# Loads of a pair at the first step in every batch, sums inverted a step later, and a longer run of unread products before the first expert

## The chip, the cores and the metric

One core of one Trainium2 chip runs the whole program; the other cores are idle. The metric is the device time of one execution in microseconds (us). TensorE (PE, with its weight loads PEld), VectorE (DVE), ScalarE (ACT), GpSimd (POOL) and SyncE (SP) each run their own instructions in order. Most transfers are issued by SP, some by ACT, the indirect ones by POOL.

## The reference

The input `x` has four batches of 1024 positions and 256 columns. A layer of attention with a normalization is followed by a layer of experts with a second normalization:

```
q, k, v = x wq^T, x wk^T, x wv^T             # 16 heads of 16 columns
q_embed = softplus(q) * (cos, sin of the position angles)
k_embed = softplus(k) * (cos, sin of the angles plus a bias)
x = layernorm(x + softmax(q_embed k_embed^T / 4) v wo^T)
gates = softmax(x router_w + router_b); the two best of 8 experts for each token
slots: each expert takes its first 640 tokens in order of position
y = sum over a token's experts of gate * (gelu(x w1 + b1) w2 + b2)
x = layernorm(x + y)
```

All is in float32.

## The kernel before

**Attention.** Work goes by units. A pair of heads of one batch is a unit of 8 steps; there are 8 pairs in a batch (the first four belong to the first half of the heads, the other four to the second) and 4 batches, so 256 steps in all. Pair p and step t of batch b are written (p, t) here. (The first and the last pair are cut into two units of 4 steps, which doesn't matter below.) In each step TensorE multiplies keys by queries (`key_scores`, L797), subtracts row maxima by a small product (L811), ScalarE takes exponentials (L818, two in each step, so that the start of the first of them marks the step), and TensorE multiplies the exponentials of the step before by the values (`weighted_values`, L838). The maxima are needed beforehand: `score_half` (L757) makes scores of a coming unit and VectorE reduces them to maxima (L761), four or so in every step. These score products of a unit may start at the last step of the pair two ahead of it; so they read the unit's `qk` tile from about (0, 6) or (0, 7) on if the unit is pair 2.

**The tiles of a pair.** `load_qk` (L471) brings a pair's embedded queries and keys from DRAM to a `qk` tile: 12 transfers on SP, 8 of 128 KB and 4 of 256 KB, 2 MB in all. There are three such buffers, so the tile of pair i takes the buffer of pair i - 3, and SP waits until that pair's last key scores are made. L1094 says at which step this is issued: at the first step of the pair two before it; but in the first pair of batches 1 to 3 at its fourth step (t = 3).

**Sums.** At the end of a unit `collect` (L856) sends six transfers on SP: numerators to `num` and sums to DRAM. When half of a batch's heads is done, `over_sums` (L879) runs in four pieces: it loads the sums as `den`; VectorE inverts them (L886), the result goes to DRAM (L888) and eight transfers spread it to `r` (L891); then two multiplications of `num` by `r` (L897). For the second half of the heads these pieces are placed at steps 1, 2, 5 and 6 of the first pair of the next batch (L947). `project` (L500) then multiplies by the output weights, from (0, 7) on, and VectorE adds the result (L514). For the first half of the heads the pieces stand at (4, 1), (4, 3) and two later steps; in the last batch at (4, 1), (4, 3), (4, 6) and (4, 7), where pair 6's tile is loaded at (4, 0).

**Order.** Within `tc.manual_schedule()` instructions go to the engines in the order of the program, and the table `todo` says what is added at which step.

**Experts.** After the last batch is routed, POOL scatters its rows to slots of the experts in DRAM by 16 indirect transfers (L692). `second_factors` (L703) computes `again`, the factors of the second normalization of the tokens that go to no expert. Then `slots_of(0, n=1)` (L1193) loads the 640 slots of the first expert as five tiles by five transfers on SP (L1198), which wait for all scatters; 34 products of `again` with the identity matrix go to an unread bank of PSUM (L1332, L1333; each is two records in the profile); `transposed` (L1201) turns each tile on TensorE (L1207) and ScalarE copies it (L1208); then TensorE multiplies by the first expert's weights (L1363, L1384), and so on through the eight experts.

Of the kernel before, what the change touches and what calls it, by code (L numbers as in the profile page):

```python
# [20 lines left out]
P = 128  # L21
# [7 lines left out]
def kernel(  # L29
# [18 lines left out]
    nc = tc.nc  # L48
    B, S, DIM = x.shape
    E, _, HID = w1.shape  # L50
    HD = 16
    NT = S // P
# [8 lines left out]
    ST = CAP // P  # L61
# [23 lines left out]
    again = keep.tile([P, B * NT], F32, name="again")  # L85

    ident = const.tile([P, P], F32, name="ident")
# [14 lines left out]
    with ExitStack() as actx:  # L102
# [750 lines left out]
        def by_rows(w):  # L853
            return units[w][1] < B - 1 or units[w][2] == 0
# [24 lines left out]
        def over_sums(b, f):  # L879

            num = nums.pop((b, f))
            width = 2 * FH * HS // P
            den = small.tile([P, width], F32, tag="den", name=f"den_{b}_{f}", bufs=1)
            nc.sync.dma_start(den, sums[b, f].rearrange("n m (c s) -> (n m c) s", s=width))
            yield
            nc.vector.reciprocal(den, den)  # L886
            over = dram.tile([2, FH, HS], F32, name=f"over_{b}_{f}")
            nc.sync.dma_start(over.rearrange("n m (c s) -> (n m c) s", s=width), den)  # L888
            r = p1.tile([P, 2, HS], F32, tag="os", name=f"r_{b}_{f}")
            for m in range(FH):  # L890
                nc.sync.dma_start(  # L891
                    r[HD * m : HD * (m + 1), :, :],
                    over[:, m, :].unsqueeze(0).to_broadcast([HD, 2, HS]),
                )
            yield
            for n in range(2):
                nc.vector.tensor_tensor(num[:, n, :], num[:, n, :], r[:, n, :], ALU.mult)  # L897
                ots[b, f, n] = num[:, n, :].rearrange("p (i t) -> p i t", t=P)
                yield
# [30 lines left out]
        def at(b, p, c, f, *args):  # L930
            todo.setdefault((b * NU + p) * NT + c, []).append((f, args))

        def run(pieces):
            next(pieces, None)
# [9 lines left out]

        for b in range(1, B):
            pieces = over_sums(b - 1, 1)
            for c in (1, 2, 5, 6):  # L947
                at(b, 0, c, run, pieces)
            for j, (p, c) in enumerate(((0, 7), (1, 0), (1, 1), (1, 2))):
                at(b, p, c, project, b - 1, 1, j)  # L950
            for j, (p, c) in enumerate(((1, 2), (1, 3), (1, 4), (1, 5))):
                at(b, p, c, statistics, b - 1, j)
# [39 lines left out]
        for w in range(1, len(units)):  # L992
            rows = range(16 if units[w][4] is None else 8)
# [3 lines left out]
            before = [starts[v] for v in range(w) if units[v][0] == units[w][0] - 1]  # L997
# [91 lines left out]
        with tc.manual_schedule():  # L1089
            for n in range(NS):  # L1090
                w, c = step_of[n]
                b, p, t = n // (NU * NT), n // NT % NU, n % NT

                if t == 0 and p > 0 or t == 3 and p == 0 and b > 0 or n == NT // 2:  # L1094
                    i = n // NT + 2
                    if i < B * NU:
                        load_qk(i)
                    elif i - B * NU < 2:
                        experts[i - B * NU] = expert_weights(i - B * NU)
                if n == NS - 2:  # L1100
                    turn_back(B - 1, 1, 0)


                third_last, others[0] = others[0], False
                items = [(score_half, *x) for x in ahead[n]]
                first, third, fourth, rest = items[:2], items[2:3], items[3:4], items[4:]
                if third_last:
                    third, fourth = [], third + fourth
                for f, *args in first:
                    f(*args)  # L1110
                if parts:
                    run(parts)
                    parts = None
                tiles = [key_scores(w, c, 0)]
                for f, *args in third:
                    f(*args)
                tiles.append(key_scores(w, c, 1))
                for f, *args in fourth:
                    f(*args)
                exponentials(w, c, tiles)  # L1120
                if n > 0:
                    weighted_values(*step_of[n - 1])
                for f, *args in rest:
                    f(*args)
                if n + 2 in starts:
                    parts = max_parts(starts.index(n + 2))
                    run(parts)
                if n + 1 in starts:
                    max_rows(starts.index(n + 1))
                if c == 1 and w > 0 and not by_rows(w - 1):  # L1130
                    normalize(w - 1)
                for f, args in todo.get(n, ()):
                    f(*args)
                if b > 0 and (p, t) in FINISH:
                    if b not in finishing:
                        finishing[b] = finish_batch(b - 1)
                    next(finishing[b], None)
                if n == NS - 2:
                    for j in range(2):
                        project(b, 1, j)  # L1140
                        statistics(b, j)
                    one, two = (
                        finish_batch(b, rotate=True, lo=lo, n=NT // 2) for lo in (0, NT // 2)
                    )
                elif n == NS - 1:
                    run(one)
            weighted_values(*step_of[NS - 1])


        with tc.manual_schedule():  # L1150
            b, n = B - 1, NT // 2
# [28 lines left out]
    with ExitStack() as mctx:  # L1180
# [9 lines left out]
        b2_sb = mconst.tile([P, E, DIM], F32, name="b2_sb")  # L1190
        nc.scalar.dma_start(b2_sb.rearrange("p e d -> p (e d)"), b2.partition_broadcast(P))

        def slots_of(e, by=nc.sync, n=ST):  # L1193

            s_sb = m2.tile([P, ST, ROW], F32, tag="slots", name=f"slots_{e}")
            rows = slots_in[e * CAP : (e + 1) * CAP, :].rearrange("(t p) d -> p t d", p=P)
            for t in range(0, ST, n):
                by.dma_start(s_sb[:, t : t + n, :], rows[:, t : t + n, :])  # L1198
            return s_sb

        def transposed(e, s_sb, t):  # L1201

            if t == 0:
                s_ts[e] = m2.tile([P, KC, CAP], F32, tag="slots_t", name=f"slots_t_{e}")
            ps = ps_t.tile([P, KC, P], F32, tag="t", name=f"st_{e}_{t}")
            for k in range(KC):
                nc.tensor.transpose(ps[:, k, :], s_sb[:, t, k * P : (k + 1) * P], ident)  # L1207
            nc.scalar.copy(s_ts[e][:, :, t * P : (t + 1) * P], ps)  # L1208
# [115 lines left out]

        y_views = dram_disjoint_views(y_rank, (E - 1) * ST)
        half = CAP // 2
        s_ts, tiles, before = {}, {0: slots_of(0, n=1)}, None
        with tc.manual_schedule():


            idle = ps_h.tile([P, 2, 512], F32, tag="h", name="idle")
            for _ in range(34):  # L1332
                nc.tensor.matmul(idle[0 : B * NT, 0, 0:P], again, ident, start=True, stop=True)  # L1333
            for t in range(ST):
                transposed(0, tiles[0], t)
            for e in range(E):
                w1_sb, w2_sb = experts.pop(e)
                s_sb, s_t = tiles.pop(e), s_ts.pop(e)
                if 0 < e < E - 1:
                    tiles[e + 1] = slots_of(e + 1)  # L1340
# [18 lines left out]
                for c in range(HC):  # L1359
                    ps = ps_h.tile([P, 2, 512], F32, tag="h", name=f"hp_{e}_{c}")  # L1360
                    for k in range(KC):
                        for i in range(2):
                            nc.tensor.matmul(  # L1363
                                ps[:, i, 0:half],
                                w1_sb[:, k, c * P : (c + 1) * P],
                                s_t[:, k, i * half : (i + 1) * half],
                                start=(k == 0),
                                stop=(k == KC - 1),
                            )
                    nc.scalar.activation(  # L1370
                        h_t[:, c, :].rearrange("p (i n) -> p i n", i=2),
                        ps[:, :, 0:half],
                        AF.Gelu,
                        bias=b1_sb[:, e, c : c + 1],
                    )
                    if e == 0 and c == 1:
                        tiles[1] = slots_of(1, nc.scalar)
                for t in range(ST):
                    if e + 1 < E and t > 0:
                        for i in (t - 1,) if t < ST - 1 else (t - 1, t):  # L1380
# [2 lines left out]
                    for c in range(HC):  # L1383
# [4 lines left out]
                            start=(c == 0),  # L1388
                            stop=(c == HC - 1),
# [22 lines left out]
                before = row, to  # L1412
# [70 lines left out]
```

## Time and profile before

| | |
|---|---|
| time, median of 5 runs | 1425.52 us (1420.96, 1420.99, 1425.52, 1426.52, 1428.54) |
| the profiled execution's own time | 1421.81 us |
| its span, first to last instruction | 1420.0 us |
| attention in it: first exponential to last | 43.7 to 1083.2 us |
| first product with an expert's weights | 1129.3 us |
| TensorE busy | 1370.6 us, 97% of the span |
| VectorE, ScalarE, GpSimd busy | 885.7, 738.8, 407.0 us |
| mean granted clock of TensorE | 0.987 |

Times in the views are in us from the first instruction. A row of a timeline gives start, length, engine, line, operation, names of what is written and read, count, and in brackets how long the engine had been idle before it and what ended this. PEclk is the granted share of TensorE's full clock.

### The profile page before, as it was taken

The page shows a single profiled execution, that of the slowest core. Times are in us where ns is not written, and L with a number is a line of the kernel's source. Part 1 is how long each engine was busy: PE and PEld are TensorE (multiplying, and loading weights), DVE is VectorE, ACT ScalarE, POOL GpSimd, SP SyncE. Part 2 cuts the span into 40 slices and gives each one's busy share as a digit, 9 for nine tenths or more (in the row PEclk, how much of TensorE's full clock was granted, in tenths as well). Part 3 has the DMA queues.
Part 4 walks back from the last instruction along what each step waited for, and adds up shares of the span by engine and source line. Part 5 has one row for each costly group of instructions (what it writes and reads, how often), then busy time and mean ns, then how long its engine had stood idle before and what let it go on. Part 6 is the DMA issues. An engine that isn't in the chain of part 4 may idle for free. (4 is left out here: it accounts for less than half of the span.)

```text
span 1420.0 us, 24627 instructions
## 1 busy us (share of the span) xinstructions
PE 1370.6 (97%) x9422; PEld 869.4 (61%) x9422; DVE 885.7 (62%) x1930; ACT 738.8 (52%) x1017; POOL 407.0 (29%) x427
## 2 busy tenths in 40 slices
PE   7999999999999999999999999999996699999998
PEld 4555556555665565556656555655654477777776
DVE  7766666666877666777856666877754333333335
ACT  5575666565566657546575664555564122222221
POOL 5252043340001646100064630000220414444443
PEclk9999999999999999999999999999998799999999
DMA  6687476255543755353566345223330256434311
GB/s 196 184 235 227 110 201 198 82 180 140 155 114 94 220 165 175 111 159 79 152 169 196 103 154 139 64 64 81 86 112 1 83 178 207 111 117 133 83 44 56
DMA packets 107421, 190.20 MB, mean 134 GB/s; under 512 B 19413, under 2 KB 56094, under 8 KB 107176
## 3 DMA queue, kind: packets, MB, share of 16 engines
q1 hardware_dynamic: 96792, 169.22, 41.8%
q0 software_dynamic: 8736, 16.87, 3.9%
q10 hardware_dynamic: 1776, 2.55, 0.6%
q8 instruction: 74, 1.21, 0.4%
q14 instruction: 43, 0.35, 0.1%
HBM read 118.27 MB, written 73.63 MB: 135 GB/s over the span
## 5 line engine op out<-in xcount | busy, mean ns | idle before, releaser
L761 DVE TENSOR_REDUCE nm<-s 128x1 f32<-128x512 f32 x1024 | 646.6, 683 | 254.6 <-PE s L757 246.1
L818 ACT ACTIVATE pt<-st 128x1024 f32<-128x1024 f32 x512 | 496.1, 1021 | 368.9 <-PE st L811 367.7
L757 PE MATMUL s<-qk 128*128 128x512 f32 x1024 | 381.1, 433 | 10.0 <-DMA qk<-embed_k 4.7
L797 PE MATMUL st<-qk 128*128 128x512 f32 x1024 | 303.1, 397 | 0.7 <-ACT pt L818 0.7
L838 PE MATMUL av<-pt,va 128*32 128x256 f32 x4096 | 275.1, 386 | 0.4 <-ACT pt L818 0.4
L757 PEld LDWEIGHTS s<-qk 128*128 128x128 f32 x1024 | 177.0, 188 | 113.9 <-DVE nm L761 41.5
L797 PEld LDWEIGHTS st<-qk 128*128 128x128 f32 x1024 | 182.8, 188 | 59.7 <-ACT pt L818 25.0
L838 PEld LDWEIGHTS av<-pt,va 128*32 128x32 f32 x4096 | 106.9, 109 | 107.3 <-issue 62.3
L414 POOL TENSOR_TENSOR soft_q<-y_q,soft_q 128x512 f32<-128x512 f32 x15 | 19.2, 1283 | 441.0 <-ACT soft_q L410 441.0
L692 POOL DMA_INDIRECT slots_in<-held,scatter_idx x64 | 62.7, 979 | 285.1 <-DVE scatter_idx L688 212.4
L1384 PE MATMUL op<-w,h 128*128 128x256 f32 x640 | 144.1, 379 | 0.0
L1363 PE MATMUL hp<-slots_t,w 128*128 128x320 f32 x512 | 139.3, 433 | 0.0
L1384 PEld LDWEIGHTS op<-w,h 128*128 128x128 f32 x640 | 119.4, 190 | 15.9
L811 PE MATMUL st<-mt,ones_r 2*128 2x512 f32 x1024 | 129.0, 493 | 0.0
L1363 PEld LDWEIGHTS hp<-slots_t,w 128*128 128x128 f32 x512 | 97.1, 190 | 39.9 <-ACT slots_t L1208 0.4
L811 PEld LDWEIGHTS st<-mt,ones_r 2*128 2x128 f32 x1024 | 49.0, 182 | 89.5 <-issue 88.8
L1370 ACT ACTIVATE h<-hp,b_sb 128x640 f32<-128x640 f32 x64 | 50.8, 793 | 86.1 <-PE hp L1363 86.1
L1400 ACT ACTIVATE o<-o,w 128x256 f32<-128x256 f32 x35 | 17.8, 507 | 103.2 <-issue 72.2
L1399 DVE TENSOR_TENSOR o<-op,b_sb 128x256 f32<-128x256 f32 x35 | 14.8, 424 | 84.8 <-PE op L1384 84.8
L1402 POOL DMA_INDIRECT y_rank<-o,rows x35 | 35.6, 1018 | 95.6 <-ACT slots_t L1208 43.0
L1316 POOL DMA_INDIRECT out_dram<-row,rows x40 | 40.3, 1008 | 43.8 <-DVE row L1303 11.8
L514 DVE TENSOR_TENSOR held<-po,held 128x512 f32<-128x512 f32 x32 | 22.1, 689 | 46.6 <-PE po L506 46.6
(219 smaller groups left out, 1059.4 us busy)
## 6 DMA issues: line engine op xcount, KB each, us to landing
qk<-embed_q SPq DMA_DIRECT2D x248, 128.0 KB
qk<-embed_k SPq DMA_DIRECT2D x124, 256.0 KB
embed_k<-parts_k SPq DMA_DIRECT2D x64, 256.0 KB
embed_q<-parts_q SPq DMA_DIRECT2D x64, 256.0 KB
w<-in_w_dram SPq DMA_DIRECT2D x16, 1024.0 KB
y_rank<-zero SPq DMA_DIRECT2D x8, 1024.0 KB
tab_q<-table SPq DMA_DIRECT2D x14, 512.0 KB
tab_k<-table SPq DMA_DIRECT2D x14, 512.0 KB
```

The source lines that it names most:

```text
L692: nc.gpsimd.indirect_dma_start(out=scatter_views[2 * t + k], out_offset=bass.IndirectOffsetOnAxis(ap=scatter_idx[:, k, t : t + 1], axis=0) ...
L757: nc.tensor.matmul(ps, qk[:, 2 * h, lo : lo + P], qk[:, 2 * h + 1, j * HS : (j + 1) * HS], start=True, stop=True,)
L761: nc.vector.tensor_reduce(nms[w][:, i, s, j : j + 1], ps, AX.X, ALU.max, negate=True)
L797: nc.tensor.matmul(ps[:, x, :], qk[:, 2 * h + 1, k * P : (k + 1) * P], qk[:, 2 * h, q * HS : (q + 1) * HS], start=True, stop=False,)
L811: nc.tensor.matmul(tiles[t][:, x, :], ones_r[rows, :], mts[w][rows, :], start=False, stop=True,)
L818: nc.scalar.activation(pt, tiles[t], AF.Exp)
L838: nc.tensor.matmul(av[32 * s : 32 * (s + 1), to], va[f][:, k, 2 * p + h, :], e, start=(c == 0 and n == 0), stop=(last and n == 1),)
L1316: nc.gpsimd.indirect_dma_start(out=out_views[t], out_offset=bass.IndirectOffsetOnAxis(ap=to[:, 0, t : t + 1], axis=0), in_=row[:, t, :], i ...
L1363: nc.tensor.matmul(ps[:, i, 0:half], w1_sb[:, k, c * P : (c + 1) * P], s_t[:, k, i * half : (i + 1) * half], start=(k == 0), stop=(k == KC ...
L1370: nc.scalar.activation(h_t[:, c, :].rearrange("p (i n) -> p i n", i=2), ps[:, :, 0:half], AF.Gelu, bias=b1_sb[:, e, c : c + 1],)
L1384: nc.tensor.matmul(ps, h_t[:, c, t * P : (t + 1) * P], w2_sb[:, c, :], start=(c == 0), stop=(c == HC - 1),)
L1402: nc.gpsimd.indirect_dma_start(out=y_views[e * ST + t], out_offset=bass.IndirectOffsetOnAxis(ap=to[:, 1, t : t + 1], axis=0), in_=o_sb, in ...
```

## The change

Three places change. `load_qk` is issued at the first step of every pair, the first pair of batches 1 to 3 included. There the pieces of `over_sums` move from steps 1, 2, 5, 6 to steps 1, 3, 6, 7. And at the start of the experts the unread products become 60 before the first tile's transposes and 3 before those of each of the four other tiles, 72 instead of 34, while the five slot transfers alternate between SP (tiles 0, 2, 4) and ACT (tiles 1, 3).

```diff
         for b in range(1, B):
             pieces = over_sums(b - 1, 1)
-            for c in (1, 2, 5, 6):
+            for c in (1, 3, 6, 7):
                 at(b, 0, c, run, pieces)
...
-                if t == 0 and p > 0 or t == 3 and p == 0 and b > 0 or n == NT // 2:
+                if n % NT == 0 and n > 0 or n == NT // 2:
                     i = n // NT + 2
                     if i < B * NU:
                         load_qk(i)
...
-        def slots_of(e, by=nc.sync, n=ST):
+        def slots_of(e, by=(nc.sync,), n=ST):
...
             for t in range(0, ST, n):
-                by.dma_start(s_sb[:, t : t + n, :], rows[:, t : t + n, :])
+                by[t % len(by)].dma_start(s_sb[:, t : t + n, :], rows[:, t : t + n, :])
...
-        s_ts, tiles, before = {}, {0: slots_of(0, n=1)}, None
+        s_ts, tiles, before = {}, {0: slots_of(0, (nc.sync, nc.scalar), n=1)}, None
...
-            for _ in range(34):
-                nc.tensor.matmul(idle[0 : B * NT, 0, 0:P], again, ident, start=True, stop=True)
             for t in range(ST):
+                for _ in range(3 if t else 60):
+                    nc.tensor.matmul(
+                        idle[0 : B * NT, 0, 0:P], again, ident, start=True, stop=True
+                    )
                 transposed(0, tiles[0], t)
...
-                        tiles[1] = slots_of(1, nc.scalar)
+                        tiles[1] = slots_of(1, (nc.scalar,))
```

The last line only follows the new form of the argument.

## The prediction

> **What bounds the kernel now.** I read the page first, then the timelines of TensorE, SyncE and ScalarE around the three places that the diff touches, then the granted clock there.
>
> ```profile
> PE 1370.6 (97%) x9422; PEld 869.4 (61%) x9422; DVE 885.7 (62%) x1930; ACT 738.8 (52%) x1017; POOL 407.0 (29%) x427
> ...
> PEclk9999999999999999999999999999998799999999
> ...
> L757 PE MATMUL s<-qk 128*128 128x512 f32 x1024 | 381.1, 433 | 10.0 <-DMA qk<-embed_k 4.7
> ```
>
> TensorE is busy nearly throughout, so only its idle time and its clock can be won back. The waits of the score products (L757) for a pair's tile stand out; the clock falls where attention ends. TensorE's timeline has these waits once in the first pair of batches 1, 2 and 3:
>
> ```profile
> 338.50 0.62 PE L797 MATMUL st<-qk 128*128 128x512 f32 x2
> 341.55 0.47 PE L757 MATMUL s<-qk 128*128 128x512 f32 x1 [2.43 <-DMA qk<-embed_k]
> ...
> 605.93 0.47 PE L757 MATMUL s<-qk 128*128 128x512 f32 x1 [2.18 <-issue]
> ...
> 869.06 0.47 PE L757 MATMUL s<-qk 128*128 128x512 f32 x1 [2.27 <-DMA qk<-embed_k]
> ```
>
> TensorE stands still for 2.43, 2.18 and 2.27 us. The second is put down to "issue", but has the same instruction at the same place. SyncE's queue shows why the tile is late in batch 1 (ahead of the dots), and the other order in the last batch's pair 4 (behind them):
>
> ```profile
> 321.48 0.32 SPq L884 DMA_DIRECT2D den<-sums  x1
> ...
> 325.51 3.59 SPq L891 DMA_DIRECT2D r<-over  x8
> 329.21 2.78 SPq L485 DMA_DIRECT2D qk<-embed_q  x4
> ...
> 335.22 1.10 SPq L487 DMA_DIRECT2D qk<-embed_k  x2
> ...
> 964.66 1.71 SPq L485 DMA_DIRECT2D qk<-embed_q  x4
> ...
> 969.61 1.09 SPq L487 DMA_DIRECT2D qk<-embed_k  x2
> ...
> 976.95 0.34 SPq L884 DMA_DIRECT2D den<-sums  x1
> 980.88 0.34 SPq L888 DMA_DIRECT2D over<-den  x1
> ```
>
> The tile's last transfer is issued at 336.3 and the product that reads it starts 5.2 us later. In the last batch's pair 4 the 12 loads go out ahead of the sums, from 4.9 us before the first exponential (969.55), and nothing waits. That pair is a model of the new order: loads at step 0, sums at steps 1, 3, 6, 7.
>
> **Part one, the loads.** The first pair's lost time, by step, from ScalarE's timeline in batch 1 (starts of steps 6, 7 and the next pair's 0):
>
> ```profile
> 337.10 1.94 ACT L818 ACTIVATE pt<-st 128x1024 f32<-128x1024 f32 x2 [1.54 <-PE st L811]
> ...
> 343.97 1.94 ACT L818 ACTIVATE pt<-st 128x1024 f32<-128x1024 f32 x2 [4.73 <-PE st L811]
> ...
> 349.55 1.94 ACT L818 ACTIVATE pt<-st 128x1024 f32<-128x1024 f32 x2 [2.66 <-PE st L811]
> ```
>
> Steps 6 and 7 take 12.45 us here, and 10.79 (601.73 to 612.52) and 11.17 us (864.76 to 875.93) in batches 2 and 3. In the model pair the same two steps take 7.37 us (990.55 to 997.92), without the projection that step 7 has here; a projection lengthens a step from 3.48 to 4.38 us (batch 1, pair 1, steps 1 and 3), so 8.27 us is what they need. That would save 4.18 + 2.52 + 2.90 = 9.6 us. Batch 1's larger share is the clock: right after its wait the granted clock is halved for 3.41 us.
>
> The loads move past these on SP: the six transfers of `collect`, the load of `den`, the store and the eight loads of `r`. In batch 1 SP is free at 310.1 (its last stores of embedded keys), the loads would take it until about 317, and `collect`'s first transfer is issued at 316.88 today, since it waits for ScalarE's copy: a delay of some 0.2 us. `den` is then issued about 7.4 to 7.8 us after the pair's first exponential (7.4 in the model pair), and the inversion, now at step 3, starts 0.3 us after that step's exponential (980.31 against 980.05 in the model), at 326.95 in batch 1: over 4 us for a 32 KB transfer. I cost this at nothing; the cover is those 4 us, and without it VectorE, which works in order, would hold up its maxima, and TensorE would run out of banks. `r` comes 3.5 us later and its multiplications one step (3.48 us) later, so they keep their distance.
>
> The second multiplication (0.68 us) now shares step 7 with the projection's addition (0.69 us) and four maxima (2.73 us): 4.1 us of VectorE in a step of 4.8, after a step of 3.80 in 3.48. It fits, with little slack, and the projection's bank stays occupied for 0.68 us more. No row shows all three together. Between nothing and 0.7 us for each batch, I take 0.2, near the model pair's rows, where a multiplication in either step cost nothing: 0.5 us in all. Part one: -9.1 us.
>
> **Part two, the start of the experts.** The granted clock, then TensorE:
>
> ```profile
> 1115.00:1120.30 5.30, 5.30 (x27) 4.42 (x26) 0.00 (x0) 0.00 (x0) 4.08 (x5) 0.50 0.37 132
> 1120.30:1126.00 5.70, 4.65 (x42) 4.38 (x40) 0.00 (x0) 0.00 (x0) 1.23 (x2) 1.00 0.10 26
> ```
>
> ```profile
> 1114.56 10.39 PE L1333 MATMUL idle<-ident,again 128*32 128x128 f32 x68 [4.68 <-DVE again L714]
> 1126.84 0.88 PE L1207 MATMUL st<-ident,slots 128*128 128x128 f32 x4 [1.89 <-DMA slots<-slots_in]
> 1128.18 1.31 PE L1207 MATMUL st<-ident,slots 128*128 128x128 f32 x6 [0.47 <-ACT slots_t L1208]
> 1129.33 1.16 PE L1363 MATMUL hp<-slots_t,w 128*128 128x320 f32 x3
> ```
>
> The clock is half until 1120.3. Starts of the unread records lie 0.213 us apart before that and 0.107 after. Today they end 1.9 us ahead of the first tile, and the wait after them does not lower the clock. With 60 products, 120 records, 27 run at half clock and 93 at full: 93 x 0.107 = 10.0 us after 1120.3, until 1130.3. The first tile is there at 1126.84, so it waits 3.5 us. Then follow five tiles of about 0.3 us (two products 0.14 apart) and 24 more records of 0.107 us: 1.5 + 2.6 = 4.1 us. The first expert's product starts at 1134.4 instead of 1129.33, 5.1 us later. Where the clock comes back between 3.4 and 6.8 us after the first unread product (here 5.7), this is 3.8 to 5.5 us. From there TensorE is busy without a gap until 1413, so the delay reaches the end.
>
> Two queues: SP issues the five transfers 0.46 us apart (2.24 us from 1124.61); alternating, the last leaves SP 0.9 us sooner. ACT has nothing to do until the first copy at 1127.33, so its two issues and their wait for the scatters hold up nobody. All five tiles are there before the 60 products end, so it brings nothing. Part two: +5.0 us.
>
> **Sum.** 1421.81 - 9.1 + 5.0 = 1417.7 us against the profiled execution's own time. That is among the quicker ones: the median is 3.7 us above it. From the median the sum is 1421.4. Part of that spread should go with the waits (halvings of the clock that some executions have more of), so I put the time between the two, at 1419.5.
>
> The Trainium skill ("TensorE: Matmul & The Clock Gate", HAM oscillation) says that the clock is halved only after an idle gap of about 3.4 us. By that the halving at batch 1 would not come from a 2.43 us wait, and part one would be worth some 1.5 us less. This trace differs: the halving follows that wait at once, while 2.18, 2.27 and 1.89 us had none.
>
> **Rivals.** (1) The clock. If the median execution halves its clock after all three waits and after the wait for the first tile too, it loses 1.5 us (12.45 less the other two batches' mean of 10.98) three times more than the profiled one, and the change removes all of it: 1425.5 - 9.1 - 4.5 + 5.0 = 1416.9. For it: the spread of the runs, and one halving in three here. Against: the 1.89 us wait didn't cause one. Chance 0.18. The same page (why this matters for your kernels) advises no idle gaps over about 3 us, which speaks for the unread products.
>
> (2) The sums become the wait: `den` lies behind 2 MB of tile on the same transfer engines, VectorE stands at the inversion, maxima and then TensorE with it. It decides once `den` needs more than 4.6 us. If it took 9.2 (2 MB at the 229 GB/s of 333 to 337 us), each batch would lose 4.6 us: 1421.8 + (13.8 - 9.1) + 5.0 = 1431.5 against the profiled execution, slower. Against: the model pair inverts 3.4 us after the issue of `den` without a wait. Chance 0.09.
>
> (3) The loads do not help, because the tile is late for a reason other than its issue. Then only part two is left: 1421.8 + 5.0 = 1426.8. Against: every other pair loads at step 0 and waits nowhere. Chance 0.07.
>
> **Numbers.** My case has 0.66. A measurement here can tell about 0.5%, 7.1 us: faster means below 1418.4, slower above 1432.6. My case falls between 1416 (part one without the 0.5, part two at 3.8) and 1423 (the median's level, part one at -7.6): 0.21 faster, 0.45 same. The first rival gives 0.13 faster and 0.05 same, the second 0.05 slower and 0.04 same, the third 0.06 same and 0.01 slower. Together 0.34, 0.60, 0.06. The range reaches from the first rival with the smaller cost of part two and the level of the quickest runs, 1413, to the third at the median's level less some, 1427.5.
>
> **What would show it.** Right: in the first pairs of batches 1 to 3 steps 6 and 7 take 8.3 to 9 us together, no wait of L757 for `qk`, no halved clock near 342; the unread products end 3 to 4 us after the first tile has landed, and 4 to 5.5 us more lie between `again` and the first product of L1363. Wrong: an idle VectorE ahead of L886 or L897, or TensorE waiting for maxima in step 7; or the first product of L1363 no later than now after `again`.

## The result and the profile after

The changed kernel takes 1419.39 us in the median of 34 runs (1417.59 to 1423.94); the kernel before takes 1425.28 us in the median of 63 runs. The ratio is 0.996 with a 95% interval of 0.9952 to 0.9969: about 6 us faster, which is less than the 0.5% that the prediction took as the least a measurement here can tell, though clear of zero. The forecast was 1419.5.

In the page of the changed kernel the score products have lost their wait:

```profile
span 1416.5 us, 24784 instructions
...
PE 1377.4 (97%) x9498; PEld 877.5 (62%) x9498; DVE 885.6 (63%) x1930; ACT 739.0 (52%) x1017; POOL 408.1 (29%) x427
...
L757 PE MATMUL s<-qk 128*128 128x512 f32 x1024 | 380.6, 432 | 2.5 <-DVE nm L761 0.6
```

The idle time before L757 fell from 10.0 to 2.5 us. TensorE is busy for 6.8 us more in a span 3.5 us shorter, which is the sign of added work that computes nothing. The queue of SyncE at the first pair of batch 1:

```profile
309.43 1.78 SPq L485 DMA_DIRECT2D qk<-embed_q  x4
...
314.46 1.92 SPq L487 DMA_DIRECT2D qk<-embed_k  x2
317.20 1.46 SPq L871 DMA_DIRECT2D num<-avs  x2
...
322.12 0.34 SPq L884 DMA_DIRECT2D den<-sums  x1
326.53 0.34 SPq L888 DMA_DIRECT2D over<-den  x1
```

The tile is issued 20 us sooner than before, ahead of the sums, and the inversion, whose store at 326.53 follows it at once, does not wait. Its row in VectorE's timeline has no idle time before it:

```profile
325.96 0.54 DVE L886 RECIPROCAL den<-den 128x64 f32<-128x64 f32 x1
```

ScalarE's exponentials mark steps 6, 7 and the next pair's 0:

```profile
336.18 1.94 ACT L818 ACTIVATE pt<-st 128x1024 f32<-128x1024 f32 x2 [1.56 <-PE st L811]
...
339.68 1.94 ACT L818 ACTIVATE pt<-st 128x1024 f32<-128x1024 f32 x2 [1.35 <-PE st L811]
...
344.55 1.02 ACT L818 ACTIVATE pt<-st 128x1024 f32<-128x1024 f32 x1 [2.45 <-PE st L811]
```

The two steps take 8.37 us instead of 12.45. At the start of the experts TensorE's timeline has the added products:

```profile
1106.04 14.99 PE L1333 MATMUL idle<-ident,again 128*32 128x128 f32 x120 [4.68 <-DVE again L714]
1120.96 0.44 PE L1206 MATMUL st<-ident,slots 128*128 128x128 f32 x2
1121.33 0.84 PE L1333 MATMUL idle<-ident,again 128*32 128x128 f32 x6
1122.10 0.44 PE L1206 MATMUL st<-ident,slots 128*128 128x128 f32 x2
...
1125.80 1.43 PE L1364 MATMUL hp<-slots_t,w 128*128 128x320 f32 x4
```

From the first unread product to the first product of the expert it is 19.76 us, against 14.77 before. SP issues the first tile at 1115.01. In the four profiles with two queues in which TensorE waits for this tile, the first transpose starts 2.7 to 2.9 us after that issue; so here the tile lay ready for about 3 us, an estimate, before its transpose at 1120.96.

The two profiled executions differ by 3.5 us of span, and this adds up. The start and batch 0 are 1.0 us shorter, which no edit explains (over all fourteen profiles of this study the first pair of batch 1 starts between 313.4 and 316.1 us). The three first pairs are 4.01, 2.35 and 2.45 us shorter, 8.8 in all. From the end of attention to the first unread product it is 1.3 us longer (32.68 against 31.37): the clock was halved for 3.41 us in the routing at 1075.5, which the kernel before escaped in its profile. That goes with the execution, not with the change: of the thirteen profiles with unread products four have this halving, among them `loads_alone` with the start of the experts as before, and take 32.7 to 32.8 us there; the other nine take 31.4. The start of the experts takes 5.0 us more. The rest, from the first product of the expert to the end, is 290.69 us in both.

### The profile page after: what moved, and what is told of

It is laid out like the page before. It is cut to its first block, busy times and chain, and to the rows that moved or that the text cites. A ratio compares the mean times of both kernels' runs of the same rounds, so it can differ in the third digit from the quotient of the medians.

```text
span 1416.5 us, 24784 instructions
## 1 busy us (share of the span) xinstructions
PE 1377.4 (97%) x9498; PEld 877.5 (62%) x9498; DVE 885.6 (63%) x1930; ACT 739.0 (52%) x1017; POOL 408.1 (29%) x427
## 4 chain that ended last, share of the span: by engine, by line
PE 93%; issue 2%; DVE 2%; DMA 1%; ACT 1%; POOL 1%; SPq 1%; POOLq 0%; ACTq 0%
PE s L757 18%; PE av L838 18%; PE st L797 17%; PE hp L1364 10%; PE op L1385 9%; PE st L811 8%; PE po L506 2%; PE ep_k L391 2%; PE ep_q L391 2%; PE vp L360 2%; PE mp L785 1%; PE idle L1333 1%; PE x1p L569 1%; PE st L1206 1%; PE xtp L343 1%
## 5 line engine op out<-in xcount | busy, mean ns | idle before, releaser
L757 PE MATMUL s<-qk 128*128 128x512 f32 x1024 | 380.6, 432 | 2.5 <-DVE nm L761 0.6
L757 PEld LDWEIGHTS s<-qk 128*128 128x128 f32 x1024 | 176.9, 188 | 105.6 <-DVE nm L761 41.5
```

Source lines behind the costliest of these rows:

```text
L757: nc.tensor.matmul(ps, qk[:, 2 * h, lo : lo + P], qk[:, 2 * h + 1, j * HS : (j + 1) * HS], start=True, stop=True,)
```

## The experiments

Two theories stood against each other. Mine: the gain is all in attention, and the start of the experts takes 5 us of it back. The rival, the clock: the longer run of unread products pays for itself in the median execution, because waits halve the clock there more often than in the one profiled. Each time below is a median beside runs of the kernel before on the same chip; since that kernel's median went from 1422.89 to 1426.67 us between the three groups of runs, kernels of different groups are compared by their ratios to it.

**Both attention edits alone** (`attention_part`).

```diff
-            for c in (1, 2, 5, 6):
+            for c in (1, 3, 6, 7):
...
-                if t == 0 and p > 0 or t == 3 and p == 0 and b > 0 or n == NT // 2:
+                if n % NT == 0 and n > 0 or n == NT // 2:
```

> Only the two edits in attention (loads of a pair at its first step in all batches, sums at steps 1, 3, 6, 7); the start of the experts as before. My theory: the gain of the change is here and the start of the experts takes 5 us of it back, so about 1415, 10 us below the kernel before and some 5 us below the changed kernel. In the profile: no wait of the score products for a tile, steps 6 and 7 of the first pairs 8.3 to 8.7 us, unread products end 1.5 to 3.3 us ahead of the first tile. Rival, the clock: the longer run of unread products pays for itself in the median execution, because the wait for the first tile halves the clock there; then this kernel is within 2 us of the changed one (1418 to 1421), and its runs spread as widely as those of the kernel before.

Measured: 1414.15 us, ratio 0.9917 (0.9892 to 0.9942); steps 6 and 7 of the first pairs take 8.38, 8.37 and 8.66 us. The gain is in attention. The clock had its part too, after the wait for the first tile:

```profile
1105.35 10.51 PE L1333 MATMUL idle<-ident,again 128*32 128x128 f32 x68 [4.68 <-DVE again L714]
1117.72 1.16 PE L1207 MATMUL st<-ident,slots 128*128 128x128 f32 x4 [1.86 <-DMA slots<-slots_in]
```

The granted clock in the stretch after it:

```profile
1115.00:1118.20 3.20, 1.28 (x11) 0.80 (x9) 0.00 (x0) 0.00 (x0) 0.00 (x0) 1.00 0.49 128
1118.20:1125.00 6.80, 6.48 (x16) 4.09 (x17) 4.81 (x19) 1.86 (x5) 0.00 (x0) 0.50 0.13 40
```

A wait of 1.86 us, no longer than the 1.89 of the kernel before, and the clock is half for 6.8 us behind it, through the transposes and the first 4 us of the expert's products. From the first unread product to the end this execution takes 308.0 us, against 305.5 before.

**The start of the experts alone** (`experts_part`).

```diff
-        def slots_of(e, by=nc.sync, n=ST):
+        def slots_of(e, by=(nc.sync,), n=ST):
...
-                by.dma_start(s_sb[:, t : t + n, :], rows[:, t : t + n, :])
+                by[t % len(by)].dma_start(s_sb[:, t : t + n, :], rows[:, t : t + n, :])
...
-        s_ts, tiles, before = {}, {0: slots_of(0, n=1)}, None
+        s_ts, tiles, before = {}, {0: slots_of(0, (nc.sync, nc.scalar), n=1)}, None
...
-            for _ in range(34):
-                nc.tensor.matmul(idle[0 : B * NT, 0, 0:P], again, ident, start=True, stop=True)
             for t in range(ST):
+                for _ in range(3 if t else 60):
+                    nc.tensor.matmul(
+                        idle[0 : B * NT, 0, 0:P], again, ident, start=True, stop=True
+                    )
                 transposed(0, tiles[0], t)
```

> Only the start of the experts is changed (60 unread products, then 3 before each further tile, two queues); attention as before. My theory: 5 us slower than the kernel before, 1430, with the waits of the score products for their tiles still there, and 19 to 20 us from the first unread product to the first product with the expert's weights instead of 14.8. Rival, the clock: the same as before within 2 us, with a narrower spread.

Measured: 1429.75 us beside 1426.67, ratio 1.0025 (1.0007 to 1.0042), 12 runs from 1425.17 to 1435.09. It is slower, by 3.6 us of 1425, with 1.0 to 6.0 in the interval: no gain in itself, but not clearly the full 5. The width of its runs did not shrink either, against the rival. The three waits for the tiles are all there, and in this execution each is followed by a halved clock, where the kernel before's profile had one:

```profile
343.40:346.80 3.40, 3.40 (x22) 2.03 (x19) 0.23 (x1) 2.52 (x3) 0.00 (x0) 0.50 0.83 224
606.20:613.00 6.80, 6.58 (x31) 3.88 (x32) 1.38 (x2) 2.52 (x3) 0.00 (x0) 0.50 0.51 142
872.50:875.90 3.40, 3.40 (x24) 1.46 (x22) 1.39 (x2) 0.91 (x1) 0.00 (x0) 0.50 0.37 110
```

Steps 6 and 7 take 11.87, 13.86 and 11.90 us there, 37.6 in all against 34.4 in the kernel before: 3.2 us that come and go with the clock. That half of the rival holds, and it belongs to attention.

**The loads alone** (`loads_alone`), the sums left at steps 1, 2, 5, 6.

```diff
-                if t == 0 and p > 0 or t == 3 and p == 0 and b > 0 or n == NT // 2:
+                if n % NT == 0 and n > 0 or n == NT // 2:
```

> Only the loads go to the first step; the sums stay at steps 1, 2, 5, 6; the start of the experts as before. My theory: the sums are then loaded behind the tile's 2 MB and inverted 3.5 us earlier than in the changed kernel, with under 1 us between the issue of that load and the inversion's turn, so VectorE waits some 2 us for it in each of the three batches; the three banks of scores hide part of this, so 0 to 2 us for each batch are lost: 1415 to 1421, most likely 1419, and VectorE's row of the inversion shows a wait. Rival: the sums needn't have been moved, VectorE's wait is hidden wholly, and the time is that of both edits in attention together, within 1 us.

Measured: 1416.69 us, ratio 0.9936 (0.9911 to 0.9961). VectorE at the first pair of batch 1:

```profile
321.45 2.48 DVE L761 TENSOR_REDUCE nm<-s 128x1 f32<-128x512 f32 x4 [0.81 <-PE s L757]
325.83 0.55 DVE L886 RECIPROCAL den<-den 128x64 f32<-128x64 f32 x1 [1.89 <-DMA den<-sums]
326.30 2.41 DVE L761 TENSOR_REDUCE nm<-s 128x1 f32<-128x512 f32 x4
```

The wait that my second rival described is real once the inversion stands a step earlier: 1.89 us here and 5.6 us in the three batches. TensorE feels about 1 us of each: the first pairs take 32.13, 32.31 and 32.04 us, against 31.04, 31.06 and 31.32 with both edits. Moving the sums as well is worth that, 3.1 us by the profiles and 2.5 by the medians; the intervals of the two ratios overlap.

**Two queues, 34 products** (`attention_queues_34`): both attention edits, the new form of `slots_of`, and

```diff
-        s_ts, tiles, before = {}, {0: slots_of(0, n=1)}, None
+        s_ts, tiles, before = {}, {0: slots_of(0, (nc.sync, nc.scalar), n=1)}, None
```

> Both edits in attention and the slots of the first expert on two queues, but 34 unread products before the first tile and none between the tiles. My theory: two queues save only SP's issue of the last tiles, 0.9 us, of which the transposes see 0 to 0.5 us: within 0.7 us of both edits in attention alone, about 1414.5. Rival: the two queues bring the first tile itself sooner (both queues start at once), and the gain is 1 us or more.

Measured: 1415.51 us, ratio 0.9927 (0.9902 to 0.9952), 1.4 us above both edits alone on one queue, with intervals that overlap widely. No gain from the second queue shows. The profiles even have the first tile later, against the rival:

```profile
1119.18 0.63 PE L1207 MATMUL st<-ident,slots 128*128 128x128 f32 x4 [2.66 <-DMA slots<-slots_in]
```

SP issues this tile at 1116.36, 2.8 us before. In the four profiles with two queues in which TensorE waits for the first tile this takes 2.7 to 2.9 us, in the five with one queue 2.2 to 2.3. The later tiles make up for part of it: where the clock stays whole for all or most of the transposes, the expert's first product starts 4.9 us after the first issue with two queues, and 4.5 to 4.7 with one.

**The whole change again** (`whole_change`), beside the next three.

> The whole change again, on the same chip as the next three kernels. Theory: 5 us above both attention edits alone (1414.2), less what the 34 products lose by a halved clock behind the wait for the first tile (some 1.5 us where it happens): 1417.7 to 1419.5. First product with the expert's weights 19 to 20 us after the first unread product, no halved clock after it.

Measured: 1419.54 us, ratio 0.9958 (0.9942 to 0.9974); 19.80 us from the first unread product to the first product of the expert, no halved clock behind it, and 290.69 us from there to the end.

**Where the 5 us lie.** Both attention edits and two queues, with 60 products and none between the tiles (`attention_60_0`), then 42 and none (`attention_42_0`), then 34 and 3 (`attention_34_3`); the edits stand against the changed kernel:

```diff
-                for _ in range(3 if t else 60):
+                for _ in range(0 if t else 60):     # attention_60_0
+                for _ in range(0 if t else 42):     # attention_42_0
+                for _ in range(3 if t else 34):     # attention_34_3
```

> Both attention edits, two queues, 60 unread products before the first tile and none between tiles. Theory: the 12 products between the tiles cost 24 x 0.107 = 2.6 us of the 5, the other part is the 60 outlasting the first tile: 2.4 to 2.6 us below the whole change. Rival: ScalarE's copies (0.36 us each, two buffers) hold the transposes up as much as the products between them do, and the difference is under 1 us.

Measured: 1415.71 us, ratio 0.9932 (0.9907 to 0.9957), 3.8 us below the whole change, more than the 2.4 to 2.6 expected. The products between the tiles cost more than half of what the start of the experts takes. In TensorE's timeline:

```profile
1107.10 16.04 PE L1334 MATMUL idle<-ident,again 128*32 128x128 f32 x120 [4.68 <-DVE again L714]
1123.07 0.66 PE L1207 MATMUL st<-ident,slots 128*128 128x128 f32 x4
1123.97 0.71 PE L1207 MATMUL st<-ident,slots 128*128 128x128 f32 x4 [0.25 <-ACT slots_t L1208]
...
1125.15 5.20 PE L1365 MATMUL hp<-slots_t,w 128*128 128x320 f32 x18
```

The five tiles take 2.08 us (1123.07 to 1125.15) instead of 4.84 (1120.96 to 1125.80 in the changed kernel): 2.8 us, a little over the 2.6 worked out. The last 1.0 us of the 3.8 stays open. ScalarE's copies hold the transposes up by 0.25 and 0.19 us.

> Both attention edits, two queues, 42 unread products and none between tiles. The 34 products of three kernels ended 1.9 to 2.7 us ahead of the first tile and the clock was halved behind this wait. Theory: 8 more products are 1.7 us, the wait shrinks to 0 to 1 us, the clock stays whole, and nothing is delayed: 1.5 us below both attention edits alone, 1412.7, the quickest kernel here. Rival: the halving is not caused by the wait but by the transposes themselves, so it stays: 1414.2.

Measured: 1413.70 us, ratio 0.9918 (0.9893 to 0.9944). The wait for the first tile is 0.89 us, the clock stays whole behind it, and from the first unread product to the end it takes 304.8 us, against 305.5 to 308.0 in the six profiles with 34 products and none between the tiles. In the median this does not show against both edits alone (0.9917).

> Both attention edits, two queues, 34 unread products before the first tile and 3 between the tiles. Theory: the products between the tiles cost 2.6 us at full clock, and the wait for the first tile stays: 1416.5 to 1417. Rival: the products between the tiles keep the clock whole by themselves (transposes do not count for it), which gives 1.5 us back: 1415.3.

Measured: 1417.37 us, ratio 0.9940 (0.9920 to 0.9960), and its profile, the slowest of its eight runs, has the worst of both: a wait of 2.38 us, a clock halved for 6.8 us, and products between the tiles at half clock.

```profile
1119.39 0.66 PE L1207 MATMUL st<-ident,slots 128*128 128x128 f32 x2 [2.38 <-DMA slots<-slots_in]
1119.98 1.49 PE L1334 MATMUL idle<-ident,again 128*32 128x128 f32 x6
```

The six records take 1.49 us here and 0.84 in the changed kernel. In this execution products between the tiles do not keep the clock whole by themselves.

**The sums alone** (`sums_alone`), the loads left at the fourth step.

```diff
-            for c in (1, 2, 5, 6):
+            for c in (1, 3, 6, 7):
```

> Only the sums move to steps 1, 3, 6, 7; the loads of the first pair stay at step 3 in the program, the start of the experts is as before. Theory by the steps: the loads come as late as before, so nothing is gained: 1425. Rival, by the order of SP's queue: SP does not wait for steps but for what its instructions wait for; with the inversion at the end of step 3 the loads, issued at the start of step 3, now stand ahead of the store that waits for the inversion, and the tile's buffer is long free, so SP issues them right after the sums' load, 7 us sooner; then the tile is there in time and most of the gain is had, less what the eight loads of the inverted sums wait behind the tile's 2 MB (0 to 2 us for each batch at the multiplication): 1415 to 1419. I hold the rival likelier.

Measured: 1416.87 us, ratio 0.9951 (0.9934 to 0.9967). That is 7 us by the ratio, where the loads alone gain 9, a difference that the intervals don't tell apart; the three first pairs are as short in both profiles (96.5 us in sum, 102.4 before). SyncE's queue:

```profile
321.95 0.32 SPq L884 DMA_DIRECT2D den<-sums  x1
322.37 1.77 SPq L485 DMA_DIRECT2D qk<-embed_q  x4
...
327.38 1.09 SPq L487 DMA_DIRECT2D qk<-embed_k  x2
328.57 0.53 SPq L888 DMA_DIRECT2D over<-den  x1
334.04 3.59 SPq L891 DMA_DIRECT2D r<-over  x8
```

The loads are written at the same step as before and go out 7 us sooner, right behind the sums' load, since nothing in SP's queue holds them any more. The price is the store of the inverted sums, which is now behind 2 MB: `r` is issued 5.5 us after it instead of 1.5, and VectorE waits for it at the first multiplication, 4.6 us in three batches:

```profile
339.69 0.69 DVE L897 TENSOR_TENSOR num<-num,r 128x512 f32<-128x512 f32 x1 [1.52 <-DMA r<-over]
```

**No unread products** (`attention_0_0`): both attention edits, two queues, `range(0 if t else 0)`.

> Both attention edits, two queues, no unread products at all. What the products are worth: without them the clock is half when the first tile lands, through the transposes and until a window of 3.41 us is full of the first expert's products. Theory: the transposes take 0.5 to 1 us longer, and 3.4 to 6.8 us of the expert's products run at half clock and lose 1.7 to 3.4 us, where 34 products lose 1.5 to 3.2 us after the first tile's wait in the profiles so far: 0.5 to 2 us above both attention edits alone, so 1415 to 1416.5. Rival: the unread products are worth nothing, 1414.2.

Measured: 1414.19 us, ratio 0.9934 (0.9909 to 0.9959), 1.4 us above both attention edits alone on the same chip. The clock is half from 1082.7 for 41 us, and the transposes take 2.76 us. The second queue is a rival for part of the 1.4 us, since this kernel has it and both edits alone do not; beside the kernel with two queues and 34 products (0.9927) it is 0.0007 of the time, 1.0 us. So 34 unread products are worth about 1 us, with intervals that overlap.

**42 products on one queue** (`attention_42_one_queue`, `range(42)` in the place of `range(34)`) and **both attention edits once more** (`attention_part_again`):

> Both attention edits and 42 unread products, all five slot transfers on SP. Theory: the wait for the first tile is under 1.2 us and the clock stays whole behind it; the last tile leaves SP 0.9 us later than on two queues, which costs 0 to 0.5 us: 1413.7 to 1414.2. If the second queue matters, over 1414.7.

> Both attention edits alone once more, on the same chip as the three others, to compare them with: 1414.2. Theory: 0.5 to 1 us slower than with 42 products on one queue, because the clock is halved behind the wait for the first tile in most executions.

Measured: 1412.38 us, ratio 0.9920 (0.9895 to 0.9945), and 1412.83 us, ratio 0.9921 (0.9896 to 0.9946). The first is the lowest median of this study and some 5.5 us below the changed kernel by the ratios; but by the ratios it is level with both edits alone (0.9917, 0.9921) and with 42 products on two queues (0.9918), and the 0.5 us between the two kernels here is no difference that these runs can tell. With 42 products TensorE has no wait for the first tile here:

```profile
1104.61 12.18 PE L1333 MATMUL idle<-ident,again 128*32 128x128 f32 x84 [4.69 <-DVE again L714]
1116.72 0.80 PE L1207 MATMUL st<-ident,slots 128*128 128x128 f32 x4
...
1118.97 11.39 PE L1363 MATMUL hp<-slots_t,w 128*128 128x320 f32 x41
```

## Why the prediction was right

*The loads.* 9.6 us were to be saved at steps 6 and 7, of which 0.5 would be lost. The profile has 8.8 over the whole first pairs. The model pair was a good one: steps 6 and 7 take 8.37, 8.37 and 8.67 us where 8.27 was the sum, 0.6 us more in all. The crowded step 7 has 0.1 us of this in each batch (4.86 to 4.90 us, where 3.87 in the model pair and 0.90 for the projection make 4.77); the other 0.3 us lie in step 6 of batch 3 (3.77 us instead of 3.50), and why is open. What the prediction did not see is that the step at which the loads are written is only one way to the gain: moving the sums alone shortens the three first pairs by 5.9 us too, since it frees SP's queue, and only both edits together reach 8.8.

*The cover.* "Over 4 us" for the load of the sums: it was issued at 322.12 and the inversion stored at 326.53 without a wait. With the cover gone (the loads alone) VectorE waited, as the step said, and TensorE lost about a third (3.1 us) of what the loads had won.

*The start of the experts.* +5.0 us worked out, 4.99 in the profile, with 14.9 us until the first transpose (15.7 worked out: the clock came back after 3.6 us, not 5.7) and 4.84 for the tiles (4.1 worked out: from the start of a tile's transposes to the next products it is 0.37 us and from there to the next transposes 0.77, where 0.30 and 0.64 were taken). Two misses of 0.8 and 0.7 us cancel, which is luck. The bounds of 3.4 and 6.8 us for the clock's return were too late at the lower end: over the thirteen profiles it came back 2.8 to 6.1 us after the first unread product. Against the general case the term is too large: it was taken from an execution whose clock stayed whole after the wait for the first tile. Of the six profiles with 34 products and none between the tiles five have it halved; from the first unread product to the end these six take 306.3 us in the mean, and the three with 60 and 3 products 310.1 to 310.5. That is 4.1 us, and the experts' part alone measured 3.6.

*The level.* Against the profiled execution the sum was 1417.7, and I put the time 1.8 us above it because the median lay higher. The profile of the changed kernel took 1418.28 us and its median is 1419.39. The spread went as foreseen: 1417.59 to 1423.94 where it was 1419.88 to 1432.63. But the 1.8 us were the middle between two values and no worked-out term, and the 1.0 us at the start and the 1.3 in the routing cancel nearly; that the forecast was right to 0.1 us is luck. What the level goes with can be read from the granted clock of every run: its mean is 0.9841, 0.9841 and 0.9849 in the three groups of runs of the kernel before, 0.9870 in the profiled one, and the time follows it (correlation -0.90 to -0.96). So a usual execution has 6 to 8 us more at half clock than the profiled one, about two halvings of 3.41 us; at the 1.5 us that one cost at batch 1 this is some 3 of the 3.5 us by which the median lies above the profile.

*The clock rival.* In attention it has a share: up to three halvings, worth some 3 us, go with the waits. The mean granted clock of all runs bears this out: with both attention edits alone it is 0.9872 and 0.9878 beside 0.9841 and 0.9849, some 8.5 us less at half clock, two to three halvings. That fits with the 11 to 12 us that these edits gain by their two ratios, where the term was 9.1 and the profiles of before and after give 8.8. Which waits the halvings of a usual execution follow, only a profile could show. At the experts the rival fails: the added products prevent a halved clock, which in five profiles cost 0.2 to 1.9 us behind the expert's first product, and cost more than that. *The third rival* is refuted by the kernel with the loads alone. *The second* did not come about in the change, though its mechanism is shown.

*Left open.* The whole change and both attention edits differ by 0.0037 to 0.0041 of the time, 5.3 to 5.8 us, where the profiles give 4.1; the intervals allow either. The second queue brings the first tile 0.5 us later in the profiles; why is open, and whether it costs more than that in the median was not separated from noise.

## What to carry to other kernels

A loaded tile that is late by 2 us costs more than its wait if the wait halves the clock; look for the queue's order before its bandwidth, since an instruction that waits in SP's queue delays everything written after it, whatever step that is written at. Work that only keeps an engine's clock up must end when the data comes: in the profiles 42 products kept the clock whole, where 60 and 12 more overdid it by 5 us, though the medians don't tell 42 from 34. And when a change has a good part and a bad one, rows elsewhere in the same trace (here a model pair and the starts of the unread records) price each before anything is run.

## What the runs showed of the hardware

The granted clock changes on a grid of 3.41 us, and its place differs from run to run. In the kernel before the changes at 342.1, 345.5, 1093.0 and 1120.3 us lie 1, 219 and 8 times 3.413 us apart. I laid that grid over each trace: behind the waits for the tiles the clock was halved where TensorE had been busy for 29% (the kernel before), 49, 37 and 44% (`experts_part`) of the window that held the wait; it stayed where the wait fell across a boundary and left 61 to 72% on either side (the kernel before, batches 2 and 3). Over all windows at full clock of the fourteen profiles, from the start of attention on, half clock followed each of the 17 with TensorE busy for at most 41% and none with 60% or more. Between these both occur: the wait for the first tile left 45% in the kernel before, and the clock stayed; 44% in `attention_part` and 53% in `attention_queues_34`, and it was halved. (Transposes count as busy in these shares, and the ends of products are modelled.) So a wait of 1.75 to 2.7 us halves the clock or not by its place on the grid. The Trainium skill ("TensorE: Matmul & The Clock Gate", HAM oscillation) puts the idle gap that halves it at about 3.4 us; here 1.75 us was enough (`experts_part`, batch 1).
